# A fixed instruction order for a kernel's head, a two-operation one-hot build, and a third buffer for gathered matrices

## The chip, the cores and the metric

The kernel runs on one core of one Trainium2 chip. Its five engines each have an in-order instruction queue: TensorE (PE; its weight loads are listed as PEld), VectorE (DVE), ScalarE (ACT), GpSimd (POOL) and SyncE (SP). SP and ACT issue plain transfers, and GpSimd issues the indirect ones (gathers and scatters by a list of row numbers). The metric is the device time of one execution in microseconds, as the median of several runs.

## The reference

The input is x, 16 batches of 512 tokens with 512 features in f32. Every token carries three small indices: a pathway (of 500), a compartment (of 5, used as time step too) and a scale type (0 or 1 here, of 3). Cut to what matters:

```python
h = _ln(x, pw_g[pathway_ids], pw_b[pathway_ids])
h = _ln(h, cp_g[compartment_ids], cp_b[compartment_ids])
t = _ln(x, tm_g[time_steps], tm_b[time_steps])
m = x + _mlp_ln(memory_state, ...)[:, None, :]     # n, r alike
s = _ln(x, ms_g[scale_type], ms_b[scale_type])
w = softmax(aw)
cat = concatenate([w[0]*h, w[1]*t, w[2]*m, w[3]*n, w[4]*r, w[5]*s], axis=-1)
out = x + _mlp_ln(cat, int_W1, int_b1, int_W2, int_b2, int_g, int_be)
```

`_ln` is a layer norm over the features, and `_mlp_ln` is a dense layer, SiLU, a second dense layer and a layer norm. The first dense layer of the last step has 6 x 512 input rows and 512 outputs.

## The kernel before, in words

**Grouping.** Only the compartment and the scale type choose the vectors tm_g and ms_g, so there are 15 groups (NG), ten of which occur. Blocks t and s of the concatenation together multiply the normed x by one 512 x 512 matrix per group, the "pair matrix". The kernel sorts the tokens by group and works on sorted tokens, 128 to a tile: 64 tiles, four in each of 16 windows. A tile's matrix is that of its first token's group. Each later group's first tile of 128 tokens is also computed beforehand as an "extra tile" with that group's matrix, and its rows lie in a table `rows_2` that a token reads if its group differs from its tile's.

**The head (lines 252 to 643).** It loads weights, counts tokens by group, and finds each token's sorted position. It turns positions into token lists with one-hot rows: for each of 64 columns, lines 408 and 409 on VectorE and line 411 on GpSimd write a one-hot row pair, and a matmul at line 413 adds it up in `pn`. `at_n` is its copy, and `tok`, `i_pw`, `i_cp`, `i_w`, `i_add` are the gather lists derived from it; `pair_at` (lines 431 to 437) finds groups by 14 comparisons with group ends. Then come the three side networks (lines 389 to 566), the x matrix `wx_` (599 to 601), and the loop at 617: for each of four sets of extra tiles, gather x, take statistics, normalise and transpose in 32 x 32 blocks (`turn_v`), `spread` the result with 16 transfers into `cV`, form each pair matrix (`pair`, line 606: four VectorE operations at line 613, a store into the DRAM tensor `pair_w`), multiply (line 639), add and store. `cV` and its source `rV` have one buffer each. After it, lines 646 to 662 prepare window 0.

**The main loop (677 to 755).** Each window of four tiles takes 16 steps. `layer1` (line 212) multiplies by three matrices: X (`wx_`) in steps 0 to 3, V (the gathered pair matrix) in steps 4, 6, 8, 10, and H (`wh_`) in steps 12 to 15. Between the V steps stands `layer2` of the window before (line 228). `front_a` and `front_b` prepare H on VectorE, with one power on GpSimd (line 104) between. `x_stats`, `turn_x` and `turn_v` prepare the next window's X and V. `gather_w` (145) fetches a pair matrix into one of two buffers `vs`, by list `i_w`. If the buffer already holds this group's matrix, the list has out-of-range numbers, and nothing is fetched. `shift_x` (204) adds a vector to x on GpSimd after its other uses, `put_out` (247) scatters finished rows, and `end_hidden` finishes the window before.

**Order.** Lines 750 to 768 stand inside `tc.manual_schedule()`: each engine runs instructions in program order. The head stands outside it, and the framework's scheduler orders it. Waits between engines follow from tiles and their buffers in both.

Of the kernel before, what the change touches and what calls it, by code (L numbers as in the profile page):

```python
# [19 lines left out]
def kernel(ctx: ExitStack, tc: tile.TileContext, a: dict, out: bass.AP):  # L20
# [38 lines left out]
    xp = ctx.enter_context(tc.tile_pool(name="xp", bufs=3))  # L59
    catp = ctx.enter_context(tc.tile_pool(name="catp", bufs=1))  # L60
    vp = ctx.enter_context(tc.tile_pool(name="vp", bufs=1))
# [16 lines left out]
    vs = [const.tile([P, NC, D], F32, name=f"vs{k}") for k in range(2)]  # L78
# [42 lines left out]
    def spread(rot, blk, name):  # L121

        cat = catp.tile([P, Q, NC, P], F32, tag=f"cat{blk}", name=name)
        for q in range(Q):
            for g in range(Q):
                nc.sync.dma_start(cat[q * L : (q + 1) * L, g].rearrange("p c t -> p (c t)"),  # L126
                                  rot[g * L : (g + 1) * L, q].rearrange("p c j t -> p (c j t)"))
        return cat


    def gather_x(st):
        w = st["w"]
        st["xb"] = xb = xp.tile([P, NJ, D], F32, tag="xb", name=f"xb{w}")
        for j in range(NJ):
            gather(xb[:, j, :], x_rows, tok[:, j, w : w + 1])
# [9 lines left out]
    def gather_w(st, g):  # L145
        w = st["w"]
        st["v", g] = v = vs[g % 2]
        gather(v.rearrange("p c f -> p (c f)"), pair_w[:, :], i_w[:, g, w : w + 1],
               bounds_check=NG * P - 1, oob_is_err=False)
# [57 lines left out]
    def layer1(st, blk, g):  # L207
        if blk == "X":
            st["p1", g] = ps_1.tile([P, D], F32, tag="p1", name=f"p1_{st['w']}_{g}")
        wt = {"X": wx_, "V": st.get(("v", g)), "H": wh_}[blk]  # L210
# [41 lines left out]
    with tc.tile_pool(name="prep", bufs=1) as prep:  # L252
        idx = prep.tile([P, 3, B * NJ], I32, name="idx")
        for k, nm in enumerate(("idx_c", "idx_m", "idx_pw")):
            nc.sync.dma_start(idx[:, k, :], a[nm])
        aw = prep.tile([P, 6], F32, name="aw")
        nc.scalar.dma_start(aw, a["aw"].partition_broadcast(P))

        tg = gp.tile([P, D], F32, tag="cp", name="tg")[:NR]
        nc.scalar.dma_start(tg[:NR5], a["ct"][:, D:])  # L260
        nc.scalar.dma_start(tg[NR5:], a["ms_g"])
        ws = yp.tile([P, NC, D], F32, tag="y", name="ws")
        nc.sync.dma_start(ws, a["int_W1"][5 * D :].rearrange("(c p) n -> p c n", p=P))
        wt = rot_tile("X", "wt").rearrange("p q c j t -> p q (c j t)")
        nc.sync.dma_start(wt, a["int_W1"][D : 2 * D].rearrange("(c p) n -> p c n", p=P))
        stT, w1s, w2s, w1x = [], [], [], []
        wb = xp.tile([P, NJ, D], F32, tag="xb", name="w1s")
        at = 0
        for nm in ("mem", "noi", "res"):
            k = a[nm + "T"].shape[0]  # L270
            kk = min(k, P)
            n = k // kk
            t = prep.tile([kk, n, B], F32, name="stT" + nm)
            nc.scalar.dma_start(t, a[nm + "T"].rearrange("(c p) b -> p c b", p=kk))
            stT.append(t)
            t = wb[:kk, at : at + n, :]
            at += n
            nc.scalar.dma_start(t, a[nm + "_W1"].rearrange("(c p) f -> p c f", p=kk))
            w1s.append(t)
        b1c = prep.tile([P, 4, NC], F32, name="b1c")  # L280
        nc.scalar.dma_start(b1c, a["b1c"])
        for s, nm in enumerate(("mem", "noi", "res")):
            t = w2 if s == 2 else rot_tile("HZ"[s], "w2s" + nm).rearrange("p q c j t -> p q (c j t)")
            nc.sync.dma_start(t, a[nm + "_W2"].rearrange("(c p) f -> p c f", p=P))
            w2s.append(t)
        for s in range(3):
            t = catp.tile([P, Q, NC, P], F32, tag=f"cat{'XHZ'[s]}", name=f"w1x{s}").rearrange("p g c t -> p g (c t)")
            nc.sync.dma_start(t, a["int_W1"][(2 + s) * D : (3 + s) * D].rearrange("(c p) n -> p c n", p=P))
            w1x.append(t)
        nc.sync.dma_start(wh_, a["int_W1"][:D].rearrange("(c p) n -> p c n", p=P))  # L290
        vr = gp.tile([P, D], F32, tag="cp", name="vr")[:9]
        nc.scalar.dma_start(vr, a["vecs"][:9])
        rb2 = xnp.tile([P, D], F32, tag="xm", name="rb2")
        for s in range(3):
            nc.scalar.dma_start(rb2[s * L : (s + 1) * L], a["vecs"][3 * s].partition_broadcast(L))
        tabs = prep.tile([P, 3, NC, L], F32, name="tabs")
        nc.gpsimd.memset(tabs, 0.0)
        for k, (nm, lo, hi) in enumerate((("tm_bT", 0, NR5), ("ms_bT", NR5, NR), ("cp_bT", 0, NR5))):
            nc.sync.dma_start(tabs[:, k, :, lo:hi], a[nm].rearrange("(c p) r -> p c r", p=P))
        nc.sync.dma_start(rows, a["vecs"][9:12].partition_broadcast(P))  # L300


        def iota(name, shape, pattern, base=0, step=0):
            t = prep.tile([P] + shape, F32, name=name)
            nc.gpsimd.iota(t, pattern, base=base, channel_multiplier=step, allow_small_or_imprecise_dtypes=True)
            return t

        i_grp = iota("i_grp", [NG], [[1, NG]])
        i_col = iota("i_col", [P], [[1, P]])
        i_row = iota("i_row", [1], [[0, 1]], step=1)  # L310
        tri = prep.tile([P, P], F32, name="tri")
        nc.vector.tensor_scalar(tri, i_col, i_row, None, ALU.is_gt)
        ones = prep.tile([P, P], F32, name="ones")
        nc.vector.memset(ones, 1.0)
        nid = iota("nid", [B, NJ], [[S, B], [1, NJ]], step=NJ)
        NQ = B * NJ


        mx = prep.tile([P, 1], F32, name="mx")
        nc.vector.tensor_reduce(mx, aw, AX.X, ALU.max)  # L320
        nmx = prep.tile([P, 1], F32, name="nmx")
        nc.vector.tensor_scalar_mul(nmx, mx, -1.0)
        ex = prep.tile([P, 6], F32, name="ex")
        nc.scalar.activation(ex, aw, AF.Exp, bias=nmx)
        sm = prep.tile([P, 1], F32, name="sm")
        nc.vector.tensor_reduce(sm, ex, AX.X, ALU.add)
        rsm = prep.tile([P, 1], F32, name="rsm")
        nc.vector.reciprocal(rsm, sm)
        wx = prep.tile([P, 6], F32, name="wx")
        nc.vector.tensor_scalar_mul(wx, ex, rsm)  # L330


        cmp_ = prep.tile([P, 3, NQ], F32, name="cmp_")
        nc.vector.tensor_copy(cmp_, idx)
        grp = prep.tile([P, 1, NQ], F32, name="grp")
        nc.vector.scalar_tensor_tensor(grp[:, 0, :], cmp_[:, 1, :], float(NR5), cmp_[:, 0, :], ALU.mult, ALU.add)
        v3 = vp.tile([P, NC, D], F32, name="v3")
        work = [t.rearrange("p c f -> p (c f)")[:, : NG * NQ] for t in (*vs, v3)]
        of_grp, run, tmp = work

        def by_grp(t):
            return t.rearrange("p (g q) -> p g q", g=NG)

        nc.vector.tensor_tensor(by_grp(of_grp), grp.to_broadcast([P, NG, NQ]),
                                i_grp.unsqueeze(2).to_broadcast([P, NG, NQ]), ALU.is_equal)
        nc.vector.tensor_tensor_scan(run, of_grp, of_grp, 0.0, ALU.add, ALU.max)
        upto = prep.tile([P, NG + 1], F32, name="upto")
        nc.vector.memset(upto[:, :1], 0.0)
        nc.vector.tensor_copy(upto[:, 1:], by_grp(run)[:, :, NQ - 1])
        cnt = prep.tile([P, NG], F32, name="cnt")  # L350
        nc.vector.tensor_sub(cnt, upto[:, 1:], upto[:, :NG])
        pc = ps_2.tile([P, 2, NG], F32, tag="p2", name="pc")
        nc.tensor.matmul(pc[:, 0, :], tri, cnt, start=True, stop=True)
        nc.tensor.matmul(pc[:, 1, :], ones, cnt, start=True, stop=True)
        tot = prep.tile([P, NG], F32, name="tot")
        nc.vector.tensor_copy(tot, pc[:, 1, :])
        ends = prep.tile([P, NG], F32, name="ends")
        nc.vector.tensor_tensor_scan(ends, tot, tot, 0.0, ALU.add, ALU.max)
        begs = prep.tile([P, NG], F32, name="begs")
        nc.vector.tensor_sub(begs, ends, tot)  # L360
        base = prep.tile([P, NG], F32, name="base")
        nc.vector.tensor_sub(base, pc[:, 0, :], upto[:, :NG])
# [6 lines left out]
        def row_col(pos, n, tag):  # L369
# [12 lines left out]
            nc.vector.tensor_copy(f, t)  # L382
            nc.vector.tensor_add(f[:, 1], f[:, 1], f[:, 2])
            return f[:, 0], f[:, 1]

        prow, pcol = row_col(pos, NQ, "t")


# [265 lines left out]
    for j in range(3):  # L654
        gather_h(st, j)
# [166 lines left out]
```

## Time and profile before

| | us |
|---|---|
| median of 3 runs (1262.82 to 1265.24) | 1262.93 |
| the profiled execution | 1262.96 |
| its span | 1261.1 |
| first X product of window 0 starts | 237.74 |
| first X product of window 1 starts | 283.71 |
| last H product of window 15 ends | 1216 |
| mean granted TensorE clock | 0.907 of full |
| moved by DMA | 232.24 MB, of it 127.45 by the software queue |

The span runs from the first to the last instruction. A row of the page's group list has the line, engine and operation, the tiles written and read with their shapes and the count, then the total busy time and the mean of one in ns, then the idle time of that engine just before these instructions and who ended most of it. In a timeline a row has the start, the length, the engine, the line and in brackets the idle time before it. The page's own slices give the course of the span in fortieths:

```
PE   6924436799798979898979898898969798969955
DVE  6768886238767686767676767677667676766433
POOL 3973332165564556455656554656454556454412
```

(Each digit is the busy share in tenths.) The first seven or eight slices are the head.

### The profile page before, as it was taken

The numbers are of one execution on the slowest core, as the hardware profiler recorded it, in microseconds if no ns is written. First come the engines' busy times: TensorE is split into PE (matmuls) and PEld (weight loads), VectorE is DVE, ScalarE is ACT, GpSimd is POOL, SyncE is SP. The second block draws the span as 40 slices with busy tenths as digits, with TensorE's granted clock in tenths as the row PEclk, the third lists the DMA queues.
The fourth block names the chain that finished last, engine by engine and source line by source line (L and its number), as shares of the span: only waits on it lengthen the run. The fifth ranks groups of instructions, "written<-read, shape, count | busy, mean of one in ns | idle before, by whom it ended". The sixth has DMA issues, their size and how long they took to land. (4 is left out here: it accounts for less than half of the span.)

```text
span 1261.1 us, 10221 instructions
## 1 busy us (share of the span) xinstructions
PE 1039.2 (82%) x2502; PEld 467.5 (37%) x2502; DVE 845.4 (67%) x1702; ACT 219.3 (17%) x308; POOL 636.0 (50%) x676
## 2 busy tenths in 40 slices
PE   6924436799989798979898979898969798969955
PEld 3611212344434343434343434343424343424422
DVE  6768886238767686767676767677667676766433
ACT  1102321112111111111111111111111111111000
POOL 3973332165564556455656554656454556454412
PEclk9657777899999898989998989999989898989987
DMA  9255877676558565667575667566766566859621
GB/s 310 84 166 177 298 267 269 178 193 189 165 154 255 138 187 160 180 180 211 156 192 154 186 187 200 159 184 167 219 172 172 150 179 164 242 161 271 190 62 38
DMA packets 107026, 232.24 MB, mean 184 GB/s; under 512 B 33442, under 2 KB 33442, under 8 KB 102744
## 3 DMA queue, kind: packets, MB, share of 16 engines
q0 software_dynamic: 41312, 127.45, 34.5%
q1 hardware_dynamic: 64390, 103.17, 28.8%
q10 hardware_dynamic: 1266, 0.99, 0.3%
q8 instruction: 20, 0.33, 0.1%
q14 instruction: 38, 0.31, 0.1%
HBM read 171.25 MB, written 37.17 MB: 165 GB/s over the span
## 5 line engine op out<-in xcount | busy, mean ns | idle before, releaser
L212 PE MATMUL p<-vs,cV 128*128 128x512 f32 x512 | 256.4, 648 | 81.7 <-DMA vs<-pair_w,i_w 81.7
L228 PE MATMUL p<-w,cZ 128*128 128x512 f32 x512 | 232.6, 598 | 13.5 <-DMA cZ<-rZ 13.5
L212 PE MATMUL p<-wx__89,cX 128*128 128x512 f32 x512 | 224.5, 597 | 7.9 <-DMA cX<-rX 7.9
L212 PE MATMUL p<-wh__90,cH 128*128 128x512 f32 x512 | 222.3, 592 | 0.0
L212 PEld LDWEIGHTS p<-vs,cV 128*128 128x128 f32 x512 | 105.5, 209 | 224.3 <-issue 130.3
L228 PEld LDWEIGHTS p<-w,cZ 128*128 128x128 f32 x512 | 98.2, 192 | 138.8 <-issue 136.9
L212 PEld LDWEIGHTS p<-wx__89,cX 128*128 128x128 f32 x512 | 98.0, 192 | 132.0 <-issue 125.0
L247 POOL DMA_INDIRECT out<-y,tok x60 | 64.1, 1068 | 157.9 <-issue 41.6
L212 PEld LDWEIGHTS p<-wh__90,cH 128*128 128x128 f32 x512 | 97.3, 190 | 122.5 <-issue 118.4
L198 ACT ACTIVATE pw<-pw,nmh,rsh 128x512 f32<-128x512 f32 x64 | 52.0, 813 | 474.4 <-DVE nmh L109 469.5
L109 DVE SCALAR_TENSOR_TENSOR nmh<-mvh,rsh 128x1 f32<-128x1 f32 x64 | 49.3, 771 | 113.4 <-POOL rsh L104 113.4
L92 POOL DMA_INDIRECT vs<-pair_w,i_w x64 | 66.8, 1043 | 100.7 <-PE p L212 88.9
L204 POOL TENSOR_TENSOR xb<-xb,rows 128x512 f32<-128x512 f32 x64 | 80.7, 1269 | 8.6 <-ACT xm L169 8.2
L169 ACT ACTIVATE xm<-xb,mnm,mrs 128x512 f32<-128x512 f32 x64 | 48.7, 805 | 205.1 <-DVE rV L118 98.7
L199 DVE TENSOR_TENSOR pw<-pw,cp 128x512 f32<-128x512 f32 x64 | 45.1, 705 | 55.5 <-ACT pw L198 54.6
L104 POOL TENSOR_TENSOR rsx<-vex,mhalf 128x4 f32<-128x4 f32 x20 | 21.0, 1048 | 121.5 <-DVE vex L102 121.5
L92 POOL DMA_INDIRECT pw<-in_pw,i_pw x64 | 69.1, 1079 | 19.6 <-issue 15.4
L92 POOL DMA_INDIRECT xb<-in_x,tok x64 | 62.6, 979 | 28.5 <-issue 20.0
L92 POOL DMA_INDIRECT cp<-cp_rows,i_cp x64 | 63.8, 996 | 21.6 <-issue 18.3
L92 POOL DMA_INDIRECT add<-rows,i_add x64 | 65.7, 1026 | 17.5 <-issue 16.9
L218 ACT ACTIVATE add<-add 128x512 f32<-128x512 f32 x64 | 40.3, 630 | 177.2 <-DVE add L217 151.3
L639 PE MATMUL pe<-vs,cVe 128*128 128x512 f32 x72 | 37.7, 679 | 40.5 <-DMA cVe<-rVe 40.5
(212 smaller groups left out, 1198.7 us busy)
## 6 DMA issues: line engine op xcount, KB each, us to landing
cH<-rH SPq DMA_DIRECT2D x256, 64.0 KB
cX<-rX SPq DMA_DIRECT2D x256, 64.0 KB
cV<-rV SPq DMA_DIRECT2D x256, 64.0 KB
cZ<-rZ SPq DMA_DIRECT2D x256, 64.0 KB
pair_w<-vs SPq DMA_DIRECT2D x10, 1024.0 KB
pair_w<-v SPq DMA_DIRECT2D x5, 1024.0 KB
cVe<-rVe SPq DMA_DIRECT2D x64, 64.0 KB
rows<-adde SPq DMA_DIRECT2D x14, 256.0 KB
```

The costliest lines, as they stand in the source:

```text
L92: nc.gpsimd.indirect_dma_start(dst, None, table, bass.IndirectOffsetOnAxis(ap=idx, axis=0), **kw)
L104: nc.gpsimd.tensor_tensor(rs[:p], ve[:p], mhalf[:p, :n], ALU.pow)
L109: nc.vector.scalar_tensor_tensor(nm, mv[:, :, 0], -1.0, rs, ALU.mult, ALU.mult)
L169: nc.scalar.activation(t, st["xb"][:, j, :], AF.Identity, bias=st[nm][:, j : j + 1], scale=st[rs][:, j : j + 1])
L198: nc.scalar.activation(pw[:, :D], pw[:, :D], AF.Identity, bias=nm, scale=rs)
L199: nc.vector.tensor_mul(pw[:, :D], pw[:, :D], cp)
L204: nc.gpsimd.tensor_add(st["xb"][:, j, :], st["xb"][:, j, :], rows[:, 2, :])
L212: nc.tensor.matmul(st["p1", g], st["c" + blk][:, g, c, :], wt[:, c, :], start=(blk == "X" and c == 0), stop=(blk == "H" and c == NC - 1))
L218: nc.scalar.activation(t, t, AF.Silu)
L228: nc.tensor.matmul(p2, st["cZ"][:, j, c, :], w2[:, c, :], start=(c == 0), stop=(c == NC - 1))
L247: nc.gpsimd.indirect_dma_start(out_rows, bass.IndirectOffsetOnAxis(ap=tok[:, j, w : w + 1], axis=0), st["y"][:, j, :], None)
L639: nc.tensor.matmul(pe, st["cV"][:, g, c, :], v[:, c, :], start=(c == 0), stop=(c == NC - 1))
```

## The change

- **Head.** `manual_schedule` now covers the whole kernel, and the head is rewritten in a fixed order. The gather of window 0's x comes as soon as `tok` is known. Its four X products stand in front of the first extra tile, and its `spread` uses the SP and ACT queues by turns. The extra tiles follow with their pieces interleaved by hand; sets 1 to 3 and window 0's x take their statistics on ScalarE (`act_stats`, with accumulating activations), set 0 on VectorE. `front_a` and `front_b` of window 0 stand behind the last extra tile.
- **One-hot.** One compare and one `scalar_tensor_tensor` on VectorE for each column; the pathway and the group are packed into one number (group x 512 + pathway), so `pair_at` is gone and groups come from shifts.
- **Buffers.** `vs` has three tiles and `xbs` three fixed ones for x (before, a pool of three, and a `v3` for the head alone). Tile t uses `vs[t % 3]`, but tile 3 uses the buffer of `wt`. The list `there` compares with the group three tiles earlier.
- **Main loop.** Window 0 has its own `first_window` for its V steps. In the others `gather_w` fetches one tile further ahead, and `shift_x` stands at steps 5 to 8.

The diff, cut:

```diff
-    vs = [const.tile([P, NC, D], F32, name=f"vs{k}") for k in range(2)]
+    vs = [const.tile([P, NC, D], F32, name=f"vs{k}") for k in range(3)]
+    xbs = [const.tile([P, NJ, D], F32, name=f"xbs{k}") for k in range(3)]
...
-    def spread(rot, blk, name):
+    def spread(rot, blk, name, queues=(nc.sync,)):
...
-    def gather_w(st, g):
-        w = st["w"]
-        st["v", g] = v = vs[g % 2]
+    def gather_w(t):
+        w, g = divmod(t, Q)
+        mats[t] = v = v03 if t == 3 else vs[t % 3]
...
-                nc.vector.tensor_scalar(oh[:, u, :P], i_col, prow[:, q : q + 1], None, ALU.is_equal)
-                nc.vector.tensor_scalar(oh[:, u, P : P + NQ], i_col[:, :NQ], pcol[:, q : q + 1],
-                                        nid.rearrange("p b j -> p (b j)")[:, q : q + 1], ALU.is_equal, ALU.mult)
-                nc.gpsimd.tensor_scalar(oh[:, u, P + NQ :], i_col[:, :NQ], pcol[:, q : q + 1],
-                                        cmp_[:, 2, q : q + 1], ALU.is_equal, ALU.mult)
+            nc.vector.tensor_scalar(oh[:, u, 0], i_col, prow[:, q : q + 1], None, ALU.is_equal)
+            nc.vector.scalar_tensor_tensor(oh[:, u, 1].rearrange("p (v q) -> p v q", v=2), i_two, pcol[:, q : q + 1],
+                                           vals[:, :, q : q + 1].to_broadcast([P, 2, NQ]), ALU.is_equal, ALU.mult)
...
+    st["cX"] = spread(st["rX"], "X", "cX0", (nc.sync, nc.scalar))
...
+    def act_stats(s, tag):
...
+        for j in range(NJ):
+            nc.scalar.activation(junk, xb[:, j, :], AF.Identity, accum_out=sums[:, 0, j : j + 1])
+        nmean = small.tile([P, NJ], F32, tag="nmean", name="nmean" + tag)
+        nc.scalar.mul(nmean, sums[:, 0], -1.0 / D)
+        for j in range(NJ):
+            nc.scalar.activation(junk, xb[:, j, :], AF.Square, bias=nmean[:, j : j + 1],
+                                 accum_out=sums[:, 1, j : j + 1])
...
+    extra_x(1)
+    pair(1)
+    extra_turn(0)
+    for g in range(Q):
+        layer1(st, "X", g)
+    act_stats(ext[1], "1")
+    pair(2)
+    pair(3)
+    ends_ = [extra(k) for k in (1, 2, 3)]
+    extra_turn(1)
+    extra_x(2)
+    act_stats(ext[2], "2")
+    pair(0)
+    gather_h(st, 1)
+    for k in (4, 5, 6, 7):
+        if ends_:
+            extra_end(ends_.pop(0))
+        pair(k)
+        ends_.append(extra(k))
+    extra_end(ends_.pop(0))
+    extra_turn(2)
+    extra_x(3)
+    act_stats(st, "0")
...
+    for k in (8, 9, 10, 11):
+        extra_end(ends_.pop(0))
+        pair(k)
+        ends_.append(extra(k))
+    act_stats(ext[3], "3")
+    extra_end(ends_.pop(0))
+    extra_turn(3)
...
+    for k in (12, 13, 14):
+        extra_end(ends_.pop(0))
+        pair(k)
+        ends_.append(extra(k))
     for j in range(NJ):
         turn_v(st, j)
     st["cV"] = spread(st["rV"], "V", "cV0")
+    nx = {"w": 1}
+    gather_x(nx)
+    for t in range(4):
+        gather_w(t)
+    for x in ends_:
+        extra_end(x)
+    for j in range(NJ):
         front_a(st, j)
         front_b(st, j)
         if j == 0:
             gather_h(st, 3)
+    st["cH"] = spread(st["rH"], "H", "cH0")
...
-        if s in (3, 4, 5, 8):
-            shift_x(st, (3, 4, 5, 8).index(s))
-
-        if s in (5, 7):
-            gather_w(st, (s - 1) // 2)
-        elif s in (9, 11) and nx is not None:
-            gather_w(nx, (s - 9) // 2)
+        if 5 <= s < 9:
+            shift_x(st, s - 5)
+
+        if s in (5, 7, 9, 11) and Q * st["w"] + (s + 1) // 2 < Q * NW:
+            gather_w(Q * st["w"] + (s + 1) // 2)
```

`pair(k)` forms pair matrix k in `vs[k % 3]` and stores it; `extra(k)` multiplies extra tile k by it; `extra_end` adds the gathered row part and stores the result; `extra_turn(e)` normalises, transposes and spreads set e; `extra_x(e)` gathers its x.

## The prediction, made before the changed kernel was run

> **Frame.** The profiled execution took 1262.96 us: a span of 1261.1 and 1.9 around it. The median of the runs shown is 1262.93, so nothing is rescaled. I write T for the start of a window (its first X product on TensorE) and n us after it as T+n.
>
> **What bounds the kernel now.** First the page, for the engines and the costliest groups:
>
> ```profile
> PE 1039.2 (82%) x2502; PEld 467.5 (37%) x2502; DVE 845.4 (67%) x1702; ACT 219.3 (17%) x308; POOL 636.0 (50%) x676
> L212 PE MATMUL p<-vs,cV 128*128 128x512 f32 x512 | 256.4, 648 | 81.7 <-DMA vs<-pair_w,i_w 81.7
> L411 POOL TENSOR_SCALAR oh<-i_col,rft,cmp__187 128x64 f32<-128x64 f32 x64 | 40.1, 648 | 10.8 <-DVE rft L383 10.8
> ```
>
> TensorE has the most work. One group waits 81.7 us, always for a pair matrix. The TensorE timeline places it (start, length, idle before): the X product that opens window 4, then the V products, of which the third waits:
>
> ```profile
> 464.48 13.90 PE L212 MATMUL p<-wx__89,cX 128*128 128x512 f32 x32
> ...
> 495.41 6.64 PE L212 MATMUL p<-vs,cV 128*128 128x512 f32 x8 [3.30 <-DMA vs<-pair_w,i_w]
> ```
>
> A window of 16 products of 3.43 us is 54.9. Windows 1 and 15 take that; windows 2 to 14 take 58.8 to 68.4, in all 108 more than 13 x 54.9. Fourteen windows have this stall, though by the inputs' group counts only 18 of the 64 gathers fetch anything. The DMA totals agree: the software queue's 127.45 MB less 108.5 for all other gathers leaves 18.9 MB, 18 matrices. So the stall is mostly late issue. GpSimd's timeline says why:
>
> ```profile
> 457.33 1.47 POOL L92 DMA_INDIRECT pw<-in_pw,i_pw  x1 [0.19 <-issue]
> ...
> 460.37 1.15 POOL L247 DMA_INDIRECT out<-y,tok  x1 [0.30 <-issue]
> 465.32 0.99 POOL L247 DMA_INDIRECT out<-y,tok  x1 [3.80 <-issue]
> 468.81 1.37 POOL L247 DMA_INDIRECT out<-y,tok  x1 [2.50 <-DVE pw L186]
> 472.76 0.97 POOL L247 DMA_INDIRECT out<-y,tok  x1 [2.59 <-DVE mvh L98]
> 474.04 0.99 POOL L92 DMA_INDIRECT xb<-in_x,tok  x1 [0.30 <-issue]
> ...
> 478.85 1.10 POOL L104 TENSOR_TENSOR rsh<-veh,mhalf 128x1 f32<-128x1 f32 x2
> 479.92 2.47 POOL L204 TENSOR_TENSOR xb<-xb,rows 128x512 f32<-128x512 f32 x2
> 490.56 1.02 POOL L104 TENSOR_TENSOR rsx<-vex,mhalf 128x4 f32<-128x4 f32 x1 [8.16 <-DVE vex L102]
> 491.56 1.26 POOL L204 TENSOR_TENSOR xb<-xb,rows 128x512 f32<-128x512 f32 x1
> 492.98 1.06 POOL L92 DMA_INDIRECT vs<-pair_w,i_w  x1 [0.17 <-issue]
> ```
>
> The matrix's buffer was free at T+17; its gather left at T+28.5, behind GpSimd's queue: scatters of the output 3.5 to 5 us apart (in the last window the releaser of such a 2.54 us gap is the previous scatter's DMA), four x gathers, the powers that VectorE waits for, and rsx, which waits for VectorE. It landed 2.4 us later, empty.
>
> The stretches by window (us, then busy time of PE, PEld, DVE, ACT, POOL, granted clock, DMA share, GB/s) show the head:
>
> ```profile
> 26.00:67.00 41.00, 38.81 (x151) 27.45 (x152) 29.41 (x130) 4.38 (x3) 39.62 (x64) 0.72 0.36 117
> 126.00:238.00 112.00, 56.13 (x113) 23.73 (x112) 74.03 (x144) 24.48 (x33) 33.71 (x33) 0.77 0.79 273
> ```
>
> The one-hot stage is GpSimd's; in the extra tiles TensorE is busy half of the time. Window 1 starts at 283.7, window 15 ends at 1216.1, a 45.0 tail follows.
>
> **Part 1, one-hot rows.** Removed: GpSimd's 64 operations, one per 0.626 us, 40.06 in all. On VectorE a 64-wide operation becomes a 128-wide scalar_tensor_tensor, not in the trace. Its 64-wide neighbour (L436) starts every 0.204; 64 elements more cost 0.067 by the slope between L436 (64 wide, 0.27) and L613 (512 wide, 0.74): 0.27. With the 128-wide compare's 0.20 that is 0.47 per column, 30.1 for 64. [...] But the trace overlaps neighbours (L408 starts at 26.21 and takes 0.27, L409 starts at 26.40): I take 30.1. TensorE's part is 0.25 per column at its fastest and at most 0.52. The first column comes at 23.4 instead of 25.4: pair sums no longer wait behind the ph products, only for the exponentials at 16.3. The table at_n is ready at 54.9, not 66.8.
>
> **Part 2, x product first.** In program order VectorE now does: token casts (56.6), extra rows (63.7), hidden vectors (hs needs the w2s chain, 74.9), the four turns of x, so cX leaves over two queues at 80.6 to 85.9, then rows, statistics, pair(1) and turns to 95.4. The cVe spread takes 16 x 0.65 plus 2.1 to land: 108, where the first extra product was at 125.3. Window 0's X product (16.06, behind a 7.9 wait) now runs at about 90 to 105, under that spread. Its price without cover is 16.
>
> **Part 3, extra tiles.** Each set is 3 or 4 products of 3.43, about 2 more for the cold start, then a spread whose last 13 DMAs wait until TensorE has left the single cV (8.5 + 2.1). VectorE's fixed order adds waits: act_stats puts 8 accumulating activations ahead, not in the trace. Below, 0.63 (the Silu row), above, twice the 0.81 of norm; nearest is norm, which starts every 0.75, so I take 0.85: 7 us per set. Behind the wait are all pair() and turns. From pair(13) on extra_end(k-1) stands before pair(k), so matrix and product alternate: 3.6 + 3.4 each. Sum: 108 to 206, 98 us where it was 104.5. If stats cost nothing it is 10 less, at the upper end 15 more.
>
> **Part 4, into window 1.** The four front pairs moved behind the last extra tile. Each is 2.4 on VectorE, 0.75 for the power, 2.5 with ACT between: 5.65. The first power is queued behind four x and four matrix gathers, the latter waiting for pair(14) to land (207). So VectorE is done at 232, cH lands at 245, H ends at 260. V (218 to 233) is covered. **Window 1 starts at 260 instead of 283.7: -24.** Ends: 245 and 285.
>
> **Part 5, third buffer.** A gather issued at step s-1 is now needed five or thirteen steps later instead of three or eleven. By the same group counts 24 gathers fetch, six more. A fetch that found its buffer free needed 6.4 us from issue (1124.56 to 1130.98). Most hide behind 13 steps; tiles 23, 35, 47, 59, 63 have only T+34.3 and may stall 2 to 4. The 81.7 as such goes. What is late next is **GpSimd's own circle**: rsx to rsx took 61.7 (428.85 to 490.56). Off it come 2.9 of waits for TensorE and 2.4 in which VectorE's nmh (2.95 instead of 0.12, at 479.46) was held while two shifts ran; on it go these two shifts, moved into steps 6 and 7 (2.5; queued behind them are the pw and cp gathers), and 0.5 for powers: **about 59**, above TensorE's 54.9. The circle may run ahead 3 or 4 us per window before adds and cH become late, which windows 1 to 3 use up.
> [...] The rows differ: after 3.40, 3.58, 3.60 the eight matmuls took 3.70, after 3.30 and another 3.58 they took 6.64 and 6.44. [...] I add nothing.
>
> **Sum.** 260 + windows 1 to 3, 3 x 55 + windows 4 to 14, 11 x 59 + window 15, 55 + tail 45 + 1.9 = **1176**.
>
> **Rivals.**
> - TensorE-bound (0.20): VectorE and GpSimd adapt, all windows 55. 260 + 15 x 54.9 + 5 + 47 = 1136. For it: window 1, the only full one before, had rsx at T+16.7. Against it: that window had no older scatters.
> - The circle stays at 62 (0.19): the shifts cost what the waits saved. 260 + 110 + 13 x 62 + 47 = 1223. For it: the scatters' spacing is untouched.
> - Slower (0.07): the two moved shifts stand in GpSimd's densest stretch and hold two-input VectorE operations, as nmh was held, while more fetches lengthen the queue. Up to 5 more per window; from 65.1 per window on (260 + 110 + 13 x 65.1 + 47) the kernel is slower, at 69 it takes 1314. Against it: only one VectorE operation per window was seen held that long.
> - No gain from the head, its fixed order waiting as long as before (0.04): T1 at 284, 1200.
>
> **Numbers.** The forecast has 0.50: 1150 to 1205, by the head's ends and 58 to 60 per window. The range 1130 to 1225 takes in the first and last rivals and half of the second. A difference under 0.2% can't be told from none. Faster 0.91, same 0.02, slower 0.07.
>
> **What would show it.** L212 on vs,cV should wait well under 81.7; at_n near 55; X product of window 0 before the first extra product; window 1 near 260; rsx spacing near 59 with TensorE waiting for something that GpSimd issues (adds through cZ, cH, or tiles 4w+3). Windows of 55 throughout, or rsx still 62 apart, prove part 5 wrong; an extra stage above 115 us, part 3.

## The result and the profile after

The changed kernel takes **1217.8 us** (median of 4 runs, 1213.2 to 1222.0) against 1263.5 for the kernel before beside it: ratio 0.964, interval 0.960 to 0.967. The forecast was 1176. The direction was right and the time lies in the range, but the gain is some 45 us where 87 were forecast. The profiled execution took 1218.06 us, a span of 1216.1 and 1.9 around it.

From the page of the changed kernel, the engines and the groups that answer to those shown of before:

```profile
PE 1036.8 (85%) x2512; PEld 462.7 (38%) x2512; DVE 814.8 (67%) x1625; ACT 244.4 (20%) x376; POOL 595.1 (49%) x602
...
L229 PE MATMUL p<-w,cZ 128*128 128x512 f32 x512 | 245.5, 626 | 41.9 <-DMA cZ<-rZ 41.9
L213 PE MATMUL p<-vs,cV 128*128 128x512 f32 x504 | 239.3, 620 | 39.1 <-DMA vs<-pair_w,i_w 19.8
...
L248 POOL DMA_INDIRECT out<-y,tok x60 | 64.3, 1071 | 171.4 <-DMA out<-y,tok 45.8
```

The wait for matrices fell from 81.7 to 19.8 as the prediction wanted, but 28.6 us for cZ have come in the loop (41.9 less 13.3 in the tail, where 13.5 was all there was before). TensorE still waits; the wait has another name. The last row points to where it comes from: before its scatters of the output GpSimd stands still for 171.4 us. Of these the profile puts 45.8 down to the scatter before and the rest to operations of VectorE and others. Before the change it was 157.9, of which only 5.1 were put down to a scatter, so the names in this row settle nothing; experiments 1 and 2 do.

The TensorE timeline of the changed kernel gives the head (start, length, idle before):

```profile
90.03 13.90 PE L213 MATMUL p<-wx__83,cX 128*128 128x512 f32 x32
108.39 12.24 PE L625 MATMUL pe<-vs,cVe 128*128 128x512 f32 x24 [4.47 <-issue]
...
208.49 3.70 PE L625 MATMUL pe<-vs,cVe 128*128 128x512 f32 x8 [1.44 <-DVE vs L619]
231.45 12.38 PE L213 MATMUL p<-vs,cV 128*128 128x512 f32 x24 [19.26 <-DMA cV<-rV]
243.67 3.60 PE L213 MATMUL p<-wt,cV 128*128 128x512 f32 x8
253.85 16.56 PE L213 MATMUL p<-wh__84,cH 128*128 128x512 f32 x32 [6.58 <-DMA cH<-rH]
270.25 5.31 PE L213 MATMUL p<-wx__83,cX 128*128 128x512 f32 x12
```

Window 1 starts at 270.25 (before 283.7, forecast 260), window 15 at 1116.6 and ends at 1171.5; the tail takes 44.6. So of the 45 us some 13.5 came from the head, 31 from the loop and 0.4 from the tail. Windows 1, 2 and 15 take 54.9, windows 3 to 14 on average 61.4.

GpSimd's timeline over the end of window 2 shows the circle, from the scatters to rsx:

```profile
379.66 1.13 POOL L248 DMA_INDIRECT out<-y,tok  x1 [0.30 <-issue]
388.70 1.04 POOL L248 DMA_INDIRECT out<-y,tok  x1 [7.91 <-DVE pw L187]
392.31 0.97 POOL L248 DMA_INDIRECT out<-y,tok  x1 [2.57 <-DVE mvh L97]
396.46 0.97 POOL L248 DMA_INDIRECT out<-y,tok  x1 [3.18 <-DMA out<-y,tok]
399.55 1.00 POOL L91 DMA_INDIRECT xbs<-in_x,tok  x1 [2.12 <-issue]
...
404.38 1.10 POOL L103 TENSOR_TENSOR rsh<-veh,mhalf 128x1 f32<-128x1 f32 x2
413.28 1.02 POOL L103 TENSOR_TENSOR rsx<-vex,mhalf 128x4 f32<-128x4 f32 x1 [7.81 <-DVE vex L101]
```

From the first scatter to the first x gather it takes 20 us. VectorE is named beside the 7.91, but what the scatters share is the output tensor. In experiment 1, which takes that away, the second write of the same window waits 0.24 (the third and fourth wait 2.57 and 3.83, for VectorE's rows, by the profile):

```profile
375.02 0.60 POOL L249 DMA_DIRECT2D out<-y  x1
375.85 0.55 POOL L249 DMA_DIRECT2D out<-y  x1 [0.24 <-DMA add<-rows,i_add]
```

### The profile page after: what moved, and what is told of

It reads as the page before. It is cut to its first block, busy times and chain, and to the rows that moved or that the text cites. A ratio compares the mean times of both kernels' runs of the same rounds, so it can differ in the third digit from the quotient of the medians.

```text
span 1216.1 us, 10103 instructions
## 1 busy us (share of the span) xinstructions
PE 1036.8 (85%) x2512; PEld 462.7 (38%) x2512; DVE 814.8 (67%) x1625; ACT 244.4 (20%) x376; POOL 595.1 (49%) x602
## 3 DMA queue, kind: packets, MB, share of 16 engines
q1 hardware_dynamic: 64006, 102.64, 30.1%
## 4 chain that ended last, share of the span: by engine, by line
PE 24%; DVE 21%; DMA 18%; issue 14%; POOL 11%; SPq 9%; ACT 2%; POOLq 0%; DVEq 0%; ACTq 0%
PE p L213 11%; SPq L125 9%; PE p L229 5%; DMA add<-rows,i_add 3%; POOL xbs L91 3%; DMA cX<-rX 3%; PE pe L625 3%; DVE pw L188 3%; DMA out<-y,tok 2%; PE pn L451 2%; DMA cH<-rH 2%; DVE rZ L117 2%; DVE sth L96 2%; DVE pw L187 2%; DMA pw<-in_pw,i_pw 2%
## 5 line engine op out<-in xcount | busy, mean ns | idle before, releaser
L229 PE MATMUL p<-w,cZ 128*128 128x512 f32 x512 | 245.5, 626 | 41.9 <-DMA cZ<-rZ 41.9
L213 PE MATMUL p<-vs,cV 128*128 128x512 f32 x504 | 239.3, 620 | 39.1 <-DMA vs<-pair_w,i_w 19.8
L229 PEld LDWEIGHTS p<-w,cZ 128*128 128x128 f32 x512 | 102.0, 201 | 176.7 <-issue 175.5
L213 PEld LDWEIGHTS p<-vs,cV 128*128 128x128 f32 x504 | 99.9, 200 | 169.9 <-issue 143.9
L248 POOL DMA_INDIRECT out<-y,tok x60 | 64.3, 1071 | 171.4 <-DMA out<-y,tok 45.8
L108 DVE SCALAR_TENSOR_TENSOR nmh<-mvh,rsh 128x1 f32<-128x1 f32 x64 | 10.6, 165 | 144.0 <-POOL rsh L103 142.7
L625 PE MATMUL pe<-vs,cVe 128*128 128x512 f32 x112 | 58.7, 686 | 49.5 <-DMA rows<-adde 30.0
L91 POOL DMA_INDIRECT xbs<-in_x,tok x64 | 62.4, 975 | 72.8 <-DVE sin L486 51.7
L91 POOL DMA_INDIRECT vs<-pair_w,i_w x63 | 70.0, 1111 | 38.2 <-DMA cV<-rV 25.5
L170 ACT ACTIVATE xm<-xbs,mnm,mrs 128x512 f32<-128x512 f32 x64 | 48.7, 808 | 191.4 <-DVE mnm L166 89.1
L205 POOL TENSOR_TENSOR xbs<-xbs,rows 128x512 f32<-128x512 f32 x64 | 81.5, 1276 | 1.2
L103 POOL TENSOR_TENSOR rsx<-vex,mhalf 128x4 f32<-128x4 f32 x16 | 16.3, 1021 | 115.6 <-DVE vex L101 115.6
L91 POOL DMA_INDIRECT add<-rows,i_add x64 | 63.1, 986 | 17.2 <-issue 14.2
```

Source lines behind the costliest of these rows:

```text
L91: nc.gpsimd.indirect_dma_start(dst, None, table, bass.IndirectOffsetOnAxis(ap=idx, axis=0), **kw)
L170: nc.scalar.activation(t, st["xb"][:, j, :], AF.Identity, bias=st[nm][:, j : j + 1], scale=st[rs][:, j : j + 1])
L205: nc.gpsimd.tensor_add(st["xb"][:, j, :], st["xb"][:, j, :], rows[:, 2, :])
L213: nc.tensor.matmul(st["p1", g], st["c" + blk][:, g, c, :], wt[:, c, :], start=(blk == "X" and c == 0), stop=(blk == "H" and c == NC - 1))
L229: nc.tensor.matmul(p2, st["cZ"][:, j, c, :], w2[:, c, :], start=(c == 0), stop=(c == NC - 1))
L248: nc.gpsimd.indirect_dma_start(out_rows, bass.IndirectOffsetOnAxis(ap=tok[:, j, w : w + 1], axis=0), st["y"][:, j, :], None)
```

## The experiments

**The theory after the result:** the loop is paced by GpSimd's in-order queue; in it, scatters wait for each other, and x gathers, powers, VectorE's chain and rsx wait behind them. Rivals: the six more matrix fetches and their traffic; the place of the shifts; TensorE's cold products (after the stall at 461.08 in the changed kernel eight took 6.75 us, at a granted clock of 0.54; at 546.54, without a stall, 3.60 at 1.00).

Each kernel was timed beside the kernel before, on one chip. The circle is the way round from one rsx (a power that the next window's statistics of x need) to the next. For the reading it is cut in three at the starts of rsx, of the first scatter and of the first x gather on GpSimd's timeline, as means over the same 13 circles of each profile (us):

| kernel | median | rsx to first scatter | first scatter to x gathers | x gathers to rsx | circle |
|---|---|---|---|---|---|
| before | 1263 | 31.9 | 14.7 | 16.6 | 63.2 |
| 3: third buffer alone | 1258.3 | 30.1 | 16.4 | 16.5 | 63.0 |
| 5: shifts alone | 1237.5 | 32.2 | 15.0 | 13.8 | 61.0 |
| 4: after, shifts back | 1241.5 | 29.9 | 16.4 | 16.5 | 62.8 |
| after | 1217.8 | 31.5 | 15.9 | 13.7 | 61.1 |
| 6: after, no fetches | 1187.6 | 31.2 | 14.2 | 13.7 | 59.2 |
| 1: plain writes | 1139.4 | 32.1 | 8.6 | 14.3 | 54.9 |
| 2: later scatters | 1138.8 | 33.4 | 7.2 | 14.3 | 54.9 |

**1. No scatters.** In `put_out`:

```diff
-        nc.gpsimd.indirect_dma_start(out_rows, bass.IndirectOffsetOnAxis(ap=tok[:, j, w : w + 1], axis=0),
-                                     st["y"][:, j, :], None)
+        r = w * S + j * P
+        nc.gpsimd.dma_start(out_rows[r : r + P, :], st["y"][:, j, :])
```

> The changed kernel, but the output tiles are written by plain transfers from GpSimd to consecutive rows of the output, same bytes and same queue; the rows stay in sorted order, so this output is not the reference's. Theory (the loop is bound by GpSimd's in-order queue, whose slow part is that each scatter of the output waits for the one before it): the waits between output writes go, rsx follows rsx by about 55, windows 3 to 14 fall from 61.4 to about 55, and the kernel takes 1140 to 1160 us. Rival (the six extra matrix fetches load the DMA queues, or TensorE runs cold after its stalls): nothing that this edit touches, 1205 to 1220.

Measured 1139.4 (1137.9 to 1139.9), just under the theory's range. Windows 1 to 15 take 54.9. The theory holds: the six more fetches and the place of the shifts are as before, so neither sets the pace alone. Cold products can't be told apart here, since the stalls before them go too (granted clock 0.948 of full, 0.929 before the edit).

**2. The same scatters, later.** In `end_hidden` the two scatters go; in `step`:

```diff
             front_a(st, 2)
+            if older is not None:
+                put_out(older, 2)
         elif s == 2:
             front_a(st, 3)
+            if older is not None:
+                put_out(older, 3)
```

> The changed kernel with the third and fourth scatter of a window moved behind the x gathers and behind one power each (steps 1 and 2 instead of ahead of everything in step 0). Same instructions, same bytes, same output. Theory: the powers that VectorE waits for no longer stand behind scatters that wait for each other; circle about 53, windows bounded by TensorE at 55, 1145 to 1170 us. Rival (fetch traffic, cold clock, place of the shifts): 1205 to 1225. A third way: last_a of step 6 then waits for the late scatter, because y has one buffer, and windows stay at 60: 1195 to 1205.

Measured 1138.8 (1136.0 to 1142.4), ratio 0.903 (0.900 to 0.906), a little below the theory's range. GpSimd's timeline of this kernel:

```profile
492.11 0.95 POOL L91 DMA_INDIRECT xbs<-in_x,tok  x1 [0.30 <-issue]
493.08 0.58 POOL L103 TENSOR_TENSOR rsh<-veh,mhalf 128x1 f32<-128x1 f32 x1
493.85 1.04 POOL L248 DMA_INDIRECT out<-y,tok  x1 [0.18 <-issue]
494.92 1.11 POOL L103 TENSOR_TENSOR rsh<-veh,mhalf 128x1 f32<-128x1 f32 x1
498.57 1.04 POOL L248 DMA_INDIRECT out<-y,tok  x1 [2.54 <-DMA out<-y,tok]
502.19 1.05 POOL L103 TENSOR_TENSOR rsx<-vex,mhalf 128x4 f32<-128x4 f32 x1 [2.58 <-DVE vex L101]
```

The wait between scatters is still there (2.54), but what VectorE needs has gone ahead of it, and the last scatter waits in time that GpSimd would spend waiting for rsx. Windows 1 to 15 take 54.9: TensorE is the bound. That is the rival "TensorE-bound, 1136" of the prediction, reached by an edit that the change didn't make.

**3. The third buffer alone**, in the kernel before (`v3` as third of `vs`, tile t in buffer t mod 3, three gathered ahead):

```diff
-        st["v", g] = v = vs[g % 2]
+        mats[t] = v = (*vs, v3)[t % 3]
```

> The kernel before with only the third matrix buffer and its fetches (three matrices gathered ahead, 24 fetched instead of 18); head, one-hot rows and shifts as before. Theory: TensorE's 81.7 us behind matrices falls to about 20, but the circle of GpSimd stays near 62 because two shifts still hold nmh, so 1240 to 1252 us. Rival 1 (the third buffer is the whole gain of the loop): loop shorter by 31, 1232 or less. Rival 2 (more fetches cost what they save): 1260 to 1268.

Measured 1258.3 (1254.2 to 1262.9), ratio 0.996 (0.993 to 0.999): 6 us, below what the theory gave it and nearest to rival 2 (the fetches cost what they save); the theory's figure for the matrix wait (20 us) was wrong too. The groups by line, with the third buffer under a name of its own:

```profile
L230 PE MATMUL p<-w,cZ 128*128 128x512 f32 x512 | 234.5, 602 | 30.2 <-DMA cZ<-rZ 30.2
L214 PE MATMUL p<-vs,cV 128*128 128x512 f32 x344 | 164.8, 625 | 20.1 <-DMA vs<-pair_w,i_w 19.5 <-issue 0.7
L214 PE MATMUL p<-v,cV 128*128 128x512 f32 x168 | 86.7, 665 | 37.0 <-DMA v<-pair_w,i_w 37.0
```

Matrices are still waited for 56.5 us, and the wait for cZ rose by 17. In the table the stretch in which GpSimd waited for a buffer is 1.8 shorter and that of the scatters 1.7 longer.

**4. The shifts back**, in the changed kernel:

```diff
-        if 5 <= s < 9:
-            shift_x(st, s - 5)
+        if s in (3, 4, 5, 8):
+            shift_x(st, (3, 4, 5, 8).index(s))
```

> The changed kernel with the four shift_x back at steps 3, 4, 5 and 8. Prediction's step: 2.4 us of held nmh comes back and 2.5 us of shifts leave the circle, so no change within 10 us (1208 to 1228). Rival 1 (the moved shifts were what freed VectorE): 13 windows by 2.4, 1240 to 1250. Rival 2 (the moved shifts only load GpSimd's densest stretch): 13 windows by 2.5 the other way, 1180 to 1190.

Measured 1241.5 (1238.3 to 1243.9): 23.7 us slower than the change. Rival 1 is right. VectorE's timeline of this kernel, and then of the changed one at the same place:

```profile
529.97 2.95 DVE L108 SCALAR_TENSOR_TENSOR nmh<-mvh,rsh 128x1 f32<-128x1 f32 x1 [10.65 <-POOL rsh L103]
```

```profile
523.79 0.16 DVE L108 SCALAR_TENSOR_TENSOR nmh<-mvh,rsh 128x1 f32<-128x1 f32 x1 [8.90 <-POOL rsh L103]
```

The one-column operation took 2.95 us while two shifts (2.48) ran on GpSimd, and 0.16 where none ran. The stretch from the x gathers to rsx is 2.8 longer in every circle. Experiment 5, the same edit in the other kernel, gives the same 2.8.

**5. The shifts alone**, the same edit the other way round in the kernel before.

> The kernel before with only the four shift_x moved to steps 5 to 8; two matrix buffers, head and one-hot rows as before. Theory (the held nmh was worth about 2.8 us per window and the shifts cost 1.7 behind rsx): the circle shrinks by 1 to 2 us in 13 windows, 1240 to 1252 us. Rival 1: with two buffers the late matrices set the windows and the moved shifts put their gathers 1.3 us later still, so nothing is won or some lost, 1262 to 1282. Rival 2 (the shifts alone bring the 24 us that they bring beside the third buffer): 1236 to 1242.

Measured 1237.5 (1235.3 to 1243.4), ratio 0.981 (0.977 to 0.984): 25 us, so rival 2, the same gain with two buffers as with three. The theory's 1 to 2 us per circle was just short of the 2.2 in the table.

**6. No fetches.** In the changed kernel `there` is set to 1 from window 1 on, so that 20 gathers skip their rows and the products use the matrix that is there.

```diff
+    nc.vector.memset(there[:, :, 1:], 1.0)
```

> The changed kernel in which, from window 1 on, every matrix gather skips all its rows, as gathers of a matrix that is already there do; 20 fetches are left out and the products use whatever matrix is in the buffer, so this output is not the reference's. Theory: the longer spacing of the scatters in windows with fetches goes, every circle is 59.4, the loop is some 22 us shorter, 1190 to 1200 us. Rival 1 (fetches lie wholly hidden, the 61.1 has another cause): 1213 to 1222. Rival 2 (fetches also slow the other transfers that TensorE waits for): 1172 to 1188.

Measured 1187.6 (1185.6 to 1193.8): the median is 2.4 us below the theory's range, at the edge of rival 2's. By the profiles window 1 starts 3.0 us earlier, although the head is the same, and the loop from window 1 on is 27.4 shorter; the circle's 1.9 us account for 25 of these (13 x 1.9). GpSimd's timeline of this kernel at the place shown of the changed one:

```profile
376.63 1.12 POOL L248 DMA_INDIRECT out<-y,tok  x1 [0.30 <-issue]
381.34 0.99 POOL L248 DMA_INDIRECT out<-y,tok  x1 [3.58 <-issue]
385.17 0.97 POOL L248 DMA_INDIRECT out<-y,tok  x1 [2.84 <-DVE mvh L97]
389.17 0.97 POOL L248 DMA_INDIRECT out<-y,tok  x1 [3.03 <-DMA out<-y,tok]
392.26 1.00 POOL L91 DMA_INDIRECT xbs<-in_x,tok  x1 [2.12 <-issue]
```

The second scatter waits 3.58 instead of 7.91. So most of what the fetches cost is not TensorE's own wait for them: the likely way is that the first scatter lands later and the chain of scatters carries the delay to rsx (landing times were not read). TensorE's 19.8 us for matrices go as well, but its wait for cZ rises from 41.9 to 49.5. From the first scatter to the x gathers, the table sorts the kernels whose scatters stand in one row by their fetches: 14.2 with none in the loop, 14.7 and 15.0 with 18 in all, 15.9 to 16.4 with 24.

**7. One-hot rows back** to two 64-wide operations, the second on GpSimd:

```diff
-            nc.vector.scalar_tensor_tensor(oh[:, u, 1]...)
+            nc.vector.tensor_scalar(oh[:, u, 1, :NQ], ... vals[:, 0, q : q + 1], ...)
+            nc.gpsimd.tensor_scalar(oh[:, u, 1, NQ:], ... vals[:, 1, q : q + 1], ...)
```

> The changed kernel with the one-hot rows as before: two 64-wide operations, the second of them on GpSimd. Prediction's step 1: the table at_n comes about 10 us later (54 to 64), the whole head moves with it, 1225 to 1231 us. Rival: something else in the head (weights that land, the hidden vectors) is as late, so that the first extra product moves by less than 3 us and the time stays at 1214 to 1222.

Measured 1223.1 (1222.2 to 1228.9), between the two. The products that use the table at_n start 9.2 us later (63.1 against 53.9), the first extra product 8.3, window 1 6.8, and 5.3 are left at the end: each stage of the head has a little room.

**8. The X product of window 0 behind the extra tiles** (`layer1(st, "X", g)` moved ahead of the turns for cV0).

> The changed kernel with window 0's X product moved from ahead of the extra tiles to ahead of window 0's V product, where TensorE waits 19.3 us for cV. Theory: that wait covers the 13.9 us of the product, window 1 still starts at about 270, 1213 to 1223 us. The prediction's price of 16 us without cover would give 1230 to 1236.

Measured 1219.4 (1218.7 to 1224.5), no change that can be told. Window 1 starts at 267.4. TensorE waits for cV0 either way, 6.1 us instead of 19.3: putting the product first bought nothing that these runs can show.

**9 and 10. Overlapping the head.** On top of experiment 2: pairs 12 to 14 in one go, cV0 into cX's tile, the fronts interleaved ahead of the matrix gathers, and spreads over two queues (the last cVe, cV0 and cH0; in the second kernel the other cVe and the last cZ too).

```diff
-        s["cV"] = spread(s["rV"], "V", f"cVe{e}")
+        s["cV"] = spread(s["rV"], "V", f"cVe{e}", (nc.sync, nc.scalar) if e == 3 else (nc.sync,))
```

> The kernel with the later scatters (1138.8), and in its head: the pair matrices 12 to 14 built in one go while VectorE waits for the last cVe, the last cVe and cV0 spread over two queues, cV0 into the tile of cX so that it needn't wait for TensorE to leave cV, and window 0's four front pairs behind the pairs, interleaved, ahead of the matrix gathers. Theory (window 1 started at 270 because V and H of window 0 came one after the other behind the extra tiles: 19 us for cV, then 6 for cH): window 1 starts at 245 to 252 instead of 265.7, all windows stay at 55, 1118 to 1126 us. Rival: the matrix gathers wait for the last pair to land and for VectorE's fronts, so window 1 starts at 258 or later, 1130 us or more.

> The same, and in addition all four cVe spreads and the last window's cZ are issued from two queues (SyncE's and ScalarE's) instead of one. Theory (a spread is 16 issues of about 0.65 us one after the other, 10 us, with TensorE waiting for it): 4 to 5 us less in the tail and up to 4 us less for each of the cVe that TensorE waits for, 1105 to 1116 us. Rival: ScalarE's issues hold its statistics back, or the transfers themselves take the time, so nothing is gained over the other kernel.

Measured 1150.9 and 1166.9: both worse than experiment 2, both theories wrong. SyncE's queue in the first of them:

```profile
185.31 8.52 SPq L125 DMA_DIRECT2D cVe<-rVe  x8
...
229.24 13.28 SPq L125 DMA_DIRECT2D cH<-rH  x8
244.30 3.70 SPq L634 DMA_DIRECT2D rows<-adde  x3
```

and GpSimd's timeline:

```profile
251.92 0.97 POOL L91 DMA_INDIRECT add<-rows,i_add  x1 [19.82 <-DMA rows<-adde]
```

Eight issues took 8.5 us, and ScalarE's eight beside them 9.0, where SyncE alone took 10.0 for sixteen in experiment 2; ScalarE stood idle for 9.85 us before its next normalisation. And the extra tiles' last sums stood behind cH on SyncE, for which window 1's first adds waited 19.8 us. A third fault shows on TensorE's timeline of the same kernel: the matrix gathers, now behind the fronts on GpSimd, left only at 227, and V waited for them:

```profile
232.81 5.88 PE L213 MATMUL p<-vs,cV 128*128 128x512 f32 x8 [22.21 <-DMA vs<-pair_w,i_w]
```

Window 1 started at 279.9 in the first kernel and at 298.3 in the second.

**11 and 12. The same without these faults.** 11 has only experiment 2, the three pairs in one go and cZ over two queues in the tail; 12 has in addition cV0 early, in cX's tile and on SyncE alone, matrix gathers ahead of the interleaved fronts, and the sums ahead of cH.

```diff
-    for k in (12, 13, 14):
-        extra_end(ends_.pop(0))
-        pair(k)
-        ends_.append(extra(k))
+    extra_end(ends_.pop(0))
+    for k in (12, 13, 14):
+        pair(k)
+        ends_.append(extra(k))
```

> The kernel with the later scatters (1138.8) with two small edits: pair matrices 12 to 14 built one after the other while VectorE waits for the last cVe (before, 13 and 14 waited for the products ahead of them), and the last window's cZ spread over two queues, which alone shortened the tail by about 3.3 us. Theory: the extra tiles end 3.5 us earlier and window 1 with them, the tail is 3.3 shorter, 1130 to 1134 us. Rival (the last cVe is held by the three matrix writes on SyncE and by their traffic): only the tail's part, 1135 to 1137.

> The same two edits, and V of window 0 prepared behind those pairs on SyncE alone, into the tile of cX; its matrix gathers ahead of the fronts, the fronts interleaved, and the last sums of the extra tiles written before cH is spread (in the kernel with the head overlapped the sums stood behind cH on SyncE, and the first gather of add waited 19.8 us for them). Theory: V starts at about 212 instead of 227, H at about 234, window 1 at 250 to 256 instead of 265.7, 1118 to 1126 us. Rival (VectorE's 27 us from the last front to window 0's first add, or GpSimd's queue, keep window 1 at 262 or later): 1131 or more.

Measured 1128.1 (1124.6 to 1129.7) and **1125.3** (1123.4 to 1128.4), ratio of the latter to the kernel before 0.892 (0.889 to 0.895). TensorE's timeline of 12:

```profile
191.41 12.09 PE L625 MATMUL pe<-vs,cVe 128*128 128x512 f32 x24 [12.98 <-DMA cVe<-rVe]
213.29 13.10 PE L213 MATMUL p<-vs,cV 128*128 128x512 f32 x24 [9.79 <-DMA cV<-rV]
226.22 3.60 PE L213 MATMUL p<-wt,cV 128*128 128x512 f32 x8
239.75 16.95 PE L213 MATMUL p<-wh__84,cH 128*128 128x512 f32 x32 [9.94 <-issue]
256.54 13.90 PE L213 MATMUL p<-wx__83,cX 128*128 128x512 f32 x32
```

V starts at 213 as expected, H almost six us later than expected, and window 1 at 256.5, at the edge of its band; the time is within its own. 11 gained 10.7 us where 6.8 were expected. In 11, V starts only at 224.9, yet window 1 at 258.1: the start of V hardly decides. The two kernels' ranges overlap: that cV0 early helps at all is not settled.

## Why the forecast was right in direction and 42 us short

- **One-hot rows: right.** The products run from 23.8 to 53.5, 29.65 us for 64 columns (forecast 30.1). The two operations last 0.281 and 0.346 on average; laid end to end they would take 40.1. They overlap, as the prediction read it from two rows of before: in the changed kernel the first compare starts at 23.22 and takes 0.28, its neighbour starts at 23.43. Of the whole, experiment 7 makes this part worth some 5 us.
- **X product and first extra product: right** (90.0 to 103.9, and 108.4). The prediction did not say that this order is worth nothing that can be told (experiment 8).
- **Extra tiles: the term of the head that was too small, 104 instead of 98.** They end at 212, not 206. The statistics on ScalarE were priced rightly: 0.63 or 0.72 for the activation and 0.19 for its accumulator, 0.75 and 0.85 from start to start. Where the 6 us lie was not tried; TensorE's waits ahead of the last three sets are 12.2, 15.7 and 14.3.
- **Into window 1: forecast 260, measured 270.25, the chain right and its beginning late.** V was covered, as forecast: it ended at 247.3, and TensorE then waited 6.58 for cH. (cV0 landed at 231 instead of 218: TensorE left the shared tile six us later, and the spread took some seven more.) What set window 1 is the other chain of the prediction: the last pair matrix lands, the matrix gathers leave, then come the first power, four fronts, cH and H. GpSimd's timeline:

```profile
215.32 1.01 POOL L91 DMA_INDIRECT vs<-pair_w,i_w  x1 [25.50 <-DMA cV<-rV]
...
220.25 0.58 POOL L103 TENSOR_TENSOR rsh<-veh,mhalf 128x1 f32<-128x1 f32 x1
```

  The gathers left at 215.3, 4.9 us after SyncE issued the store of the last pair matrix, where the prediction had it landed at 207. (In the 25.5 us of waiting cV is named; in experiment 2, with the same head, it is the store of the pair matrix.) From there the links were as long as forecast: cH landed 38.5 us later (forecast 38), and H took 16.4 (forecast 15). So of the 10.25 us some 8.3 are the lateness of the last pair, which is built in the order of the extra tiles; these ended 6 us late. The same head started window 1 at 265.7 and 267.2 in experiments 2 and 6, so a few us of the miss are spread between executions.
- **The circle: the mechanism right, its size off by 1.7 us (61.1 instead of 59.4).** The forecast took 61.7, read from one circle of before (428.85 to 490.56). The mean of 13 was 63.2, lifted by long ones of up to 67.6. That is 1.5 of the 1.7. From it came 2.9 (TensorE), 2.4 (nmh) and on it 2.5 and 0.5, net -2.3; measured -2.1. In circles without fetches the forecast is met (59.2 in experiment 6). That the net came so near is luck: the next point shows that its terms were not those. The circle was also rounded down to 59, windows 3 to 14 are 0.3 longer than the mean circle, and window 3 was put at 55: 11 x 2.4 and 6, some 32 us, and with the head's 10 the miss.
- **What made the loop's gain: wrong.** The sum let the nmh hold and the shifts cancel and left the loop's gain to the third buffer. Experiments 3 to 5 say the reverse: the shifts 24 to 25 us, the buffer 6. The hold was 2.8 rather than 2.4, and the shifts cost 1.6 rather than 2.5 behind rsx, part of them in time that GpSimd waits anyway. The buffer's 1.8 was eaten by 1.7 in the scatters, from six more fetches that the prediction counted and let "hide behind 13 steps". From TensorE they hide for the most part (19.8 us of waiting in all); GpSimd's scatters wait instead.
- **Cold products: nothing added, right as to the time.** Eight products after a stall of the loop took 3.67 to 6.75 us in the changed kernel, but rsx sets the pace (61.1 a circle, 61.4 a window). The stalls' lengths alone do not sort cold products from others, as the last section shows.
- **Rivals.** "The circle stays at 62" (1223) lies nearest in time, and its ground, the untouched spacing of the scatters, is what experiments 1 and 2 confirm; its reason, that the shifts cost what the waits saved, is refuted by experiments 4 and 5.

By parts, each a difference of medians: the kernel before to experiment 3, 6.0 us for the buffer; 3 to 4, 16.8 for the head; 4 to the changed kernel, 23.6 for the shifts.

## What to carry to other kernels

Here GpSimd's in-order queue closed a circle with other engines, and when the bound engine's wait for matrices fell from 81.7 to 19.8 us, 28.6 came back under another name (cZ). In such a case look for the longest idle row on the queue's own engine, and put what others wait for ahead of its serial chain, as experiment 2 does by moving two scatters, for 79 us. Read such a circle's length as a mean over all its turns, and cut it into stretches before pricing edits. A transfer that hardly anybody waits for can still cost: TensorE waited 19.8 us for the matrices, and without 20 of their fetches the kernel took 30.2 less, likely by way of the serial chain of scatters.

## What was not expected of the hardware

- In the kernel before and in the changed one scatters to the output tensor went out 3.5 us apart at the closest (1.0 of issue, 2.5 of waiting), although their rows never meet; plain writes of the same bytes to separate rows went without that wait (0.84 from the first to the second in experiment 1). Of the changed kernel's 60 the profile puts the wait of 15 (45.8 us) down to the scatter before. Whether the chip needs that wait or the program only asks for it was not tried.
- Two queues did not halve a spread: 8.5 and 9.0 us for the eight issues of the last cVe on each (experiment 9), 10.0 for sixteen on one (experiment 2). In the tail the wait for cZ fell from 13.3 to 10.5 (experiments 11 and 12).
- After stalls of nearly one length TensorE's products were fast or slow. From the changed kernel's TensorE timeline:

```profile
541.31 5.40 PE L213 MATMUL p<-vs,cV 128*128 128x512 f32 x8 [3.54 <-DMA vs<-pair_w,i_w]
...
724.55 6.44 PE L213 MATMUL p<-vs,cV 128*128 128x512 f32 x8 [3.37 <-DMA vs<-pair_w,i_w]
...
824.02 3.67 PE L229 MATMUL p<-w,cZ 128*128 128x512 f32 x8 [3.77 <-DMA cZ<-rZ]
```

The eight products took 5.40 us after 3.54, 6.44 after 3.37 and 3.67 after 3.77; the granted clock over them was 0.68, 0.57 and 1.00. No run here shows what decides it.
